# A graph layer on one core: batches of picks over three groups each, in place of three and two in turn

## The chip, the core and the metric

The kernel runs on one core of a Trainium2 chip. A core has five engines with a queue of instructions each: TensorE (PE in the profile, with its weight loads as PEld), VectorE (DVE), ScalarE (ACT), GpSimd (POOL) and SyncE (SP). Here SP only issues DMAs, and GpSimd issues nearly nothing but indirect DMAs, which gather rows of a table by a list of indices. The metric is the time of one execution on the device in microseconds (us), the median of several runs.

## What is computed

One layer of attention over a graph of 6250 nodes with 64 features and 206250 edges, sorted by destination, then a residual sum and a layer norm:

```python
Qh = (x @ Wq.T + bq).reshape(n, H, D)
Kh = (x @ Wk.T + bk).reshape(n, H, D)
Vh = (x @ Wv.T + bv).reshape(n, H, D)
Ee = (edge_attr @ We.T + be).reshape(-1, H, D)
score = (Kh[src] * Qh[dst] * (1.0 / np.sqrt(D)) * Ee).sum(-1)
score = jnp.exp(jnp.clip(score, -5.0, 5.0))
msg = Vh[src] * score[..., None]
wV = jax.ops.segment_sum(msg, dst, num_segments=n)
...
x = _layernorm(x + wV.reshape(n, H * D), axis=-1)
```

with 4 heads of 16 features. For each edge the keys and values of its source node are needed, `Kh[src]` and `Vh[src]`; the sources are random, and this lookup is what the change is about.

## The kernel before

The edges lie in 1612 tiles of 128 (an edge to a partition), 8 tiles to a group: 202 groups, numbered from 0. The main loop runs over the groups. Two groups make a step (the last 8 groups are steps of their own). A preamble makes a table of keys and values in DRAM, `kv_tab`, with a row for each node.

**A group's work.** TensorE transforms the edges' features (`edges`, tile `ee`), fetches the destinations' queries by a product with one-hot rows (`queries`, `qq`), and turns the product of the two (`turn`, `qe`). VectorE multiplies with the keys and sums over a head (`products`: `prod` L811, `score` L813), ScalarE takes the exponential (`weigh`), VectorE weights the values (`message`, L835). TensorE sums a step's messages by destination (`sums`, tile `room`), and VectorE adds the sum into a ring of blocks (`add`, `still` L905). The code of a group mixes the work of several groups: `edges` runs three groups ahead, one-hot rows four.

**Keys and values come in two ways.** Most tiles are gathered: GpSimd issues an indirect DMA for each tile (L295, tile `kv`), four steps ahead of its use, in lots; the first gather of a lot waits for a mark, a place that TensorE must have reached. The other way are the *picks*. For some groups the last two tiles are not gathered. A batch of picks serves four tiles, the last two of each of two adjoining groups. TensorE selects the rows of `x` for the batch's 512 edges by products with one-hot matrices, from a copy of `x` in the on-chip memory (`parts`), and transforms them. A batch goes so:

- `sources` and `second`: ScalarE and VectorE make the row and the remainder of each index (L257 to L259, L678);
- `hots` (L702): VectorE makes the one-hot matrices in seven pieces; pieces 1, 3 and 5 (tile `thin`) are made narrow and widened by ScalarE (L713). Pieces 0 to 5 cover two units of `x` each, piece 6 one unit (the row `hot<-over`);
- `picks`: 50 products of 128x512 on TensorE (tile `pick`), summed in two banks of the accumulator memory;
- `picked`: VectorE merges the two banks into the tile `x` (L728, L729). The next batch's first pick must wait for this, since it overwrites the banks;
- `picked_kv` and `place_kv`: four products with the weights (rows `ee<-w,x`), and two copies by ScalarE into the tiles `kv` (L744).

**What sets the order.** All is emitted by hand in the loop's order, and each engine runs its queue in that order. A list gives the lengths of batches in groups:

```python
LENGTHS = [3, 2]
...
BEGIN = [begin(m) for m in range(LAST)]
READY = [begin(m + 1) - 1 for m in range(LAST)]
```

Batch m runs over groups BEGIN[m] to READY[m]: before, groups 1 to 3, 4 to 5, 6 to 8, 9 to 10 and so on, to group 195. `pieces_of(g)` spreads the seven pieces over the batch's groups: 2, 2 and 3 in a batch of three, 3 and 4 in a batch of two. The picks of a piece are emitted in its group, and its one-hot matrix a group ahead. `picked` stands at the end of group READY[m], and the tiles that the batch serves are those of the groups READY[m] + 4 and READY[m] + 5.

Of the kernel before, what the change touches and what calls it, by code (L numbers as in the profile page):

```python
# [81 lines left out]
PIECES = [(k, min(k + 2, UNITS)) for k in range(0, UNITS, 2)]  # L82
assert PIECES[-1] == (UNITS - 1, UNITS)
WIDE = (1, 3, 5)
LENGTHS = [3, 2]
LEAD = 1
XG = 5

# [1 line left out]
def begin(m):  # L90

    return LEAD + m // len(LENGTHS) * sum(LENGTHS) + sum(LENGTHS[:m % len(LENGTHS)])

# [1233 lines left out]
```

## Time and profile before

| | |
|---|---|
| median of 3 runs | 2004.55 us (1999.72 to 2005.15) |
| the profiled execution | 1987.82 us |
| its span, first to last instruction | 1986.0 us |
| mean granted clock of TensorE | 0.93 |
| rate of the DMAs over the span | 103 GB/s |

The profile is of one execution. It lists each engine's busy time, groups of equal instructions with their busy time, the mean of one, and the engine's idle time ahead of them with what ended it (`<-`). A row of the timeline gives the start and duration in us, the engine, the line, the operation, what it writes and reads, and in brackets how long the engine had idled and what released it. "remote" there is a release that the profile cannot put to an instruction. Windows cut the span at given times and add up each engine's busy time inside.

### The profile page before, as it was taken

How to read it: one execution, taken by the hardware profiler on the slowest of the kernel's cores; microseconds unless marked ns; L12 is line 12 of the kernel's file. 1: busy time of each engine (PE TensorE's matmuls, PEld its weight loads, DVE VectorE, ACT ScalarE, POOL GpSimd, SP SyncE). 2: the span in 40 equal slices, each digit the busy share in tenths (PEclk: the TensorE clock that was granted, in tenths of full speed). 3: DMA queues.
4: the chain of work that ended last, by engine and by line, in shares of the span. 5: the costliest groups of instructions: out<-in, count | busy, mean ns of one | idle time of the engine just before them, and what ended most of it. 6: DMA issues, size and time to landing. Idle time of an engine off the chain costs nothing.

```text
span 1986.0 us, 24370 instructions
## 1 busy us (share of the span) xinstructions
PE 1665.1 (84%) x7369; PEld 1180.0 (59%) x7369; DVE 1515.3 (76%) x2728; ACT 1321.2 (67%) x2047; POOL 1258.1 (63%) x1310
## 2 busy tenths in 40 slices
PE   6467888988888897988788888888888888978995
PEld 5345666666566665666566666666556665656663
DVE  4366878777877786878778787878787877778886
ACT  3356767676666676767666676766766766677774
POOL 6666666666666666666666666666666666666441
PEclk9779999999999899999989999999999999999996
DMA  5543333333333333333333333333333333333320
GB/s 169 166 122 108 105 101 94 111 106 91 105 102 92 108 104 96 102 102 105 102 92 106 99 96 99 101 106 107 92 104 113 101 103 104 92 105 90 111 72 20
DMA packets 116109, 203.60 MB, mean 103 GB/s; under 512 B 54784, under 2 KB 56425, under 8 KB 115855
## 3 DMA queue, kind: packets, MB, share of 16 engines
q1 hardware_dynamic: 73932, 116.94, 20.0%
q0 software_dynamic: 41600, 83.97, 15.5%
q10 hardware_dynamic: 436, 1.04, 0.2%
q8 instruction: 60, 0.98, 0.2%
q14 instruction: 81, 0.66, 0.1%
HBM read 194.25 MB, written 7.59 MB: 102 GB/s over the span
## 4 chain that ended last, share of the span: by engine, by line
PE 52%; DVE 24%; issue 9%; ACT 7%; another core or an unknown queue 5%; DMA 1%; POOL 1%; DVEq 0%; SPq 0%; ACTq 0%; POOLq 0%
PE pick L749 32%; PE ee L749 8%; DVE hot L702 5%; PE room L749 4%; PE qe L780 3%; PE qq L749 3%; DVE x L728 2%; DVE prod L811 2%; DVE qe L835 2%; DVE score L813 2%; DVE msg L855 2%; DVE thin L702 2%; DVE still L905 1%; DMA kv<-kv_tab,src_i 1%
## 5 line engine op out<-in xcount | busy, mean ns | idle before, releaser
L295 POOL DMA_INDIRECT kv<-kv_tab,src_i x1260 | 1218.0, 967 | 671.9 <-issue 289.9
L749 PE MATMUL pick<-hot,parts 128*128 128x512 f32 x3900 | 1140.9, 436 | 123.0 <-DVE x L728 107.6
L749 PEld LDWEIGHTS pick<-hot,parts 128*128 128x128 f32 x3900 | 743.5, 199 | 427.4 <-DVE x L728 140.6
L702 DVE TENSOR_TENSOR hot<-from,still 128x1024 fp32r<-128x1024 bf16 x231 | 280.4, 1214 | 8.2 <-ACT from L257 5.5
L818 ACT ACTIVATE score<-score,five_p 128x32 f32<-128x32 f32 x203 | 64.3, 317 | 310.6 <-DVE score L813 236.7
L749 PE MATMUL ee<-et,we_sb 128*128 128x512 f32 x404 | 218.6, 623 | 46.4 <-ACT kv L744 39.3
L713 ACT ACTIVATE hot<-thin 128x1024 fp32r<-128x1024 bf16 x234 | 245.3, 1048 | 0.1
L849 ACT ACTIVATE msg<-qe 128x512 fp32r<-128x512 f32 (+1 forms) x206 | 122.8, 596 | 166.0 <-DVE qe L835 96.0
L278 ACT ACTIVATE to<-to,one_p 126x1024 bf16<-126x1024 bf16 x198 | 225.8, 1140 | 0.1
L272 ACT ACTIVATE to<-kb,minus_row 126x1024 bf16<-126x1024 uint8 x198 | 225.2, 1137 | 0.0
L728 DVE SCALAR_TENSOR_TENSOR x<-odd,upper,pick 128x512 f32<-128x512 int32 x77 | 57.4, 745 | 199.9 <-PE pick L749 85.4
L780 PE MATMUL qe<-ident,term 128*128 128x128 f32 x806 | 135.4, 294 | 72.0 <-issue 30.0
L760 ACT ACTIVATE eb<-ee,be_col 128x512 f32<-128x512 f32 x202 | 135.8, 672 | 88.7 <-PE pick L749 33.8
L780 PEld LDWEIGHTS qe<-ident,term 128*128 128x128 f32 x806 | 105.4, 152 | 123.9 <-DVE term L774 42.0
L835 DVE SCALAR_TENSOR_TENSOR qe<-weight,kv 128x512 f32<-128x512 f32 x200 | 139.9, 699 | 35.2 <-ACT weight L820 19.4
L702 DVE TENSOR_TENSOR thin<-from,still 128x1024 bf16<-128x1024 bf16 x231 | 157.1, 680 | 0.0
L811 DVE TENSOR_TENSOR prod<-kv,qe 128x512 f32<-128x512 f32 x203 | 136.5, 672 | 19.9 <-remote 10.6
L813 DVE TENSOR_REDUCE score<-prod 128x32 f32<-128x512 f32 x203 | 138.5, 682 | 7.0
L774 DVE TENSOR_TENSOR term<-eb,qq 128x512 f32<-128x512 f32 x202 | 136.6, 676 | 6.5 <-DMA qw<-q_tab 3.3
L855 DVE TENSOR_TENSOR msg<-qe,msg 128x512 fp32r<-128x512 f32 x194 | 132.2, 681 | 3.8 <-ACT eb L760 2.3
L905 DVE TENSOR_REDUCE still<-room 64x64 f32<-64x128 f32 x194 | 57.9, 298 | 95.4 <-PE pick L749 40.0
L749 PEld LDWEIGHTS room<-msg,wide 128*128 128x128 f32 x776 | 114.3, 191 | 25.0 <-issue 11.3
(167 smaller groups left out, 1525.4 us busy)
## 6 DMA issues: line engine op xcount, KB each, us to landing
et<-in_eT SPq DMA_DIRECT2D x100, 512.0 KB
kb<-key_tab SPq DMA_DIRECT2D x101, 252.0 KB
kv<-kv_tab,src_i POOLq DMA_INDIRECT x1260
srcs<-in_src_rows SPq DMA_DIRECT2D x78, 256.0 KB
qw<-q_tab SPq DMA_DIRECT2D x202, 15.8 KB
kv_tab<-kv_sb SPq DMA_DIRECT2D x4, 640.0 KB
q_tab<-q SPq DMA_DIRECT2D x5, 480.0 KB
out<-y SPq DMA_DIRECT2D x2, 512.0 KB
```

The lines of the kernel that those rows point to most:

```text
L272: nc.scalar.activation(TO[g][:, :n, :], KB.pop(g)[:, :n * P].rearrange("p (j e) -> p j e", j=n), AF.Square, bias=minus_row3[:3 * W])
L278: nc.scalar.activation(TO[g][:, :n, :], TO[g][:, :n, :], AF.Relu, bias=one_p[:3 * W], scale=-1.0)
L295: return nc.gpsimd.indirect_dma_start(out=kv_of(g)[:, j, :], out_offset=None, in_=kv_tab[:, :], in_offset=bass.IndirectOffsetOnAxis(ap=src ...
L702: nc.vector.tensor_tensor(to.rearrange("p b (a c) -> p b a c", c=2), pairs((FROM if hi < UNITS else OVER)[m])[:, None].to_broadcast(shape) ...
L713: nc.scalar.activation(*THIN.pop(0), AF.Copy)
L749: mark.append(nc.tensor.matmul(*aps, **kw))
L774: nc.vector.tensor_mul(TERM[g][:, :n], EB.pop(g)[:, :n], qq[:, :n])
L780: nc.tensor.transpose(qe[g % 2][:, 2 * k:2 * k + 2, :], TERM[g][:, k, :], ident)
L811: nc.vector.tensor_mul(prod, kv_of(g)[:, lo:hi, :C], qe[g % 2][:, lo:hi, :])
L813: nc.vector.tensor_reduce(SCORE[g], prod.rearrange("p g (h d) -> p g h d", h=H), axis=AX.X, op=OP.add)
L835: nc.vector.scalar_tensor_tensor(to.rearrange("p g (h d) -> p g h d", h=H), WEIGHT.pop(g)[:, :, :, None].to_broadcast([P, n, H, D]), LEAST ...
L855: nc.vector.tensor_sub(part_of(g, 1)[1], left, part)
```

## The change

One entry of the list of lengths goes:

```diff
 WIDE = (1, 3, 5)
-LENGTHS = [3, 2]
+LENGTHS = [3]
 LEAD = 1
 XG = 5
```

Batches now run over groups 1 to 3, 4 to 6, 7 to 9 and so on, again to group 195. By the count of instructions in the program there are 65 batches in place of 78: 3250 picks on TensorE in place of 3900, and 13 fewer of each instruction that a batch has once. Four tiles for each batch that is gone are gathered instead: 1312 gathers in the main loop in place of 1260, and with the 40 of the preamble 1352 in place of 1300.

**TensorE, second group of the second batch** (group 5), from the queries' product to the next group's first picks. The tiles `pick_758` and `pick_759` are the two banks of the picks; `ee<-et` closes a group. Before:

```order
L749 MATMUL pick_758<-hot,parts 128x512 x2
L749 MATMUL pick_759<-hot,parts 128x512 x2
L749 MATMUL pick_758<-hot,parts 128x512 x2
L749 MATMUL pick_759<-hot,parts 128x512 x2
L749 MATMUL pick_758<-hot,parts 128x512 x2
L749 MATMUL pick_759<-hot,parts 128x512 x2
L749 MATMUL pick_758<-hot,parts 128x512 x2
L749 MATMUL pick_759<-hot,parts 128x512 x2
L749 MATMUL pick_758<-hot,parts 128x512
L749 MATMUL pick_759<-hot,parts 128x512
L749 MATMUL ee<-et,we_sb 128x512
```

The same place after:

```order
L749 MATMUL pick_758<-hot,parts 128x512 x2
L749 MATMUL pick_759<-hot,parts 128x512 x2
L749 MATMUL pick_758<-hot,parts 128x512 x2
L749 MATMUL pick_759<-hot,parts 128x512 x2
L749 MATMUL ee<-et,we_sb 128x512
```

Of the 18 picks that stood here 8 are left; the rest of the batch has moved to group 6.

**VectorE, last group of a batch of three**: before, that of groups 11 to 13, from the add of an earlier step's sum to `x`.

```order
L905 TENSOR_REDUCE still<-room 64x64 x2
L911 SCALAR_TENSOR_TENSOR ring<-still,above,ring 128x64
L914 TENSOR_SCALAR ring<-still,below 128x64
L962 TENSOR_TENSOR y<-y,room 128x128
L702 TENSOR_TENSOR hot<-from,still 128x1024
L835 SCALAR_TENSOR_TENSOR qe_763<-weight,kv_67 128x512
L702 TENSOR_TENSOR thin<-from,still 128x1024
L702 TENSOR_TENSOR hot<-from,still 128x1024
L797 TENSOR_TENSOR of<-still,key 128x1024
L855 TENSOR_TENSOR msg<-qe_763,msg 128x8x64
L728 SCALAR_TENSOR_TENSOR x_760<-odd,upper,pick_758 128x512
```

After, the same stretch in a batch of three that ends in a group of the same kind, groups 7 to 9:

```order
L905 TENSOR_REDUCE still<-room 64x64 x2
L911 SCALAR_TENSOR_TENSOR ring<-still,above,ring 128x64
L914 TENSOR_SCALAR ring<-still,below 128x64
L702 TENSOR_TENSOR hot<-from,still 128x1024
L835 SCALAR_TENSOR_TENSOR qe_763<-weight,kv_70 128x512
L702 TENSOR_TENSOR thin<-from,still 128x1024
L797 TENSOR_TENSOR of<-still,key 128x1024
L855 TENSOR_TENSOR msg<-qe_763,msg 128x8x64
L728 SCALAR_TENSOR_TENSOR x_760<-odd,upper,pick_758 128x512
```

One of the pieces for the next batch (`hot` behind `thin`) no longer stands ahead of `x`: the next batch needs two pieces for its first group, not three.

**GpSimd, the gathers of five steps in a row** (the tiles `kv_66` to `kv_70` are the five buffers of a step). Before:

```order
L295 DMA kv_66<-kv_tab,src_i 128x128 x14
L295 DMA kv_67<-kv_tab,src_i 128x128 x12
L295 DMA kv_68<-kv_tab,src_i 128x128 x12
L295 DMA kv_69<-kv_tab,src_i 128x128 x14
L295 DMA kv_70<-kv_tab,src_i 128x128 x12
```

After:

```order
L295 DMA kv_66<-kv_tab,src_i 128x128 x14
L295 DMA kv_67<-kv_tab,src_i 128x128 x12
L295 DMA kv_68<-kv_tab,src_i 128x128 x14
L295 DMA kv_69<-kv_tab,src_i 128x128 x14
L295 DMA kv_70<-kv_tab,src_i 128x128 x12
```

Of five steps two were gathered with 14 tiles and three with 12; now two of every three have 14. The order of steps, the marks and the lead of four steps are as before.

## The prediction

> **What bounds the kernel now.** I read the engines' totals first, then cut the loop at its own joints. Each batch of picks ends in one VectorE instruction, `x` at L728, in the program's order a fixed place of the batch's last group; its 78 starts are the edges of the windows below.
>
> ```profile
> PE 1665.1 (84%) x7369; PEld 1180.0 (59%) x7369; DVE 1515.3 (76%) x2728; ACT 1321.2 (67%) x2047; POOL 1258.1 (63%) x1310
> PE 52%; DVE 24%; issue 9%; ACT 7%; another core or an unknown queue 5%; DMA 1%; POOL 1%; DVEq 0%; SPq 0%; ACTq 0%; POOLq 0%
> ```
>
> No engine is full, and the chain of work that ended last hops between TensorE and VectorE. The kernel before holds both kinds of batch, so it times the new one itself. First the 37 batches of three groups (first row, the last two, the sum), then the 37 of two (first, last, sum); the columns are the window, its length, and each engine's busy time with its instructions.
>
> ```profile
> core 0: us, PE busy (x) PEld busy (x) DVE busy (x) ACT busy (x) POOL busy (x), PEclk, DMA share, GB/s
> 213.13:239.91 26.78, 23.81 (x111) 16.48 (x109) 21.96 (x38) 17.01 (x27) 17.91 (x19) 0.94 0.36 106
> ...
> 1857.09:1878.28 21.19, 19.59 (x92) 13.74 (x91) 20.62 (x36) 16.33 (x27) 6.95 (x8) 1.00 0.26 78
> 1896.26:1919.82 23.56, 21.34 (x101) 15.05 (x99) 21.87 (x37) 16.92 (x28) 10.06 (x11) 1.00 0.26 79
> sum 1007.88, PE 827.49 PEld 567.51 DVE 800.37 ACT 655.88 POOL 663.66; mean PE 22.36 PEld 15.34 DVE 21.63 ACT 17.73 POOL 17.94
> ```
>
> ```profile
> 194.88:213.13 18.25, 17.44 (x72) 13.15 (x73) 14.84 (x25) 13.82 (x21) 10.51 (x11) 0.86 0.36 99
> ...
> 1878.28:1896.26 17.98, 17.51 (x83) 13.01 (x82) 14.84 (x26) 15.12 (x23) 7.55 (x8) 1.00 0.32 90
> sum 717.06, PE 667.89 PEld 491.43 DVE 563.59 ACT 538.66 POOL 455.09; mean PE 18.05 PEld 13.28 DVE 15.23 ACT 14.56 POOL 12.30
> ```
>
> A batch of three takes 1007.88/37 = 27.24 us, 9.08 a group; one of two takes 717.06/37 = 19.38 us, 9.69 a group. In the short ones TensorE is busy 18.05 of 19.38 us (93%): they are TensorE's. In the long ones it is busy 22.36 of 27.24 (82%) and VectorE 21.63 (79%): something else paces them. Who waits at the joint says what:
>
> ```profile
> 615.97 0.74 DVE L728 SCALAR_TENSOR_TENSOR x<-odd,upper,pick 128x512 f32<-128x512 int32 x1
> 616.76 3.54 PE L749 MATMUL pick<-hot,parts 128*128 128x512 f32 x8 [4.28 <-DVE x L728]
> ...
> 627.80 2.44 PE L749 MATMUL pick<-hot,parts 128*128 128x512 f32 x8
> ...
> 635.23 0.75 DVE L728 SCALAR_TENSOR_TENSOR x<-odd,upper,pick 128x512 f32<-128x512 int32 x1 [3.32 <-PE pick L749]
> ```
>
> ```profile
> 662.67 0.75 DVE L728 SCALAR_TENSOR_TENSOR x<-odd,upper,pick 128x512 f32<-128x512 int32 x1 [5.33 <-remote]
> 663.47 3.78 PE L749 MATMUL pick<-hot,parts 128*128 128x512 f32 x8 [5.20 <-DVE x L728]
> ```
>
> At 615.97 a long batch ends in an odd group: VectorE reaches `x` without idling, late, and TensorE has stood 4.28 us. At 635.23 a short batch ends: VectorE waits 3.32 us for the last pick. At 662.67 a long batch ends in an even group (8, 18, 28 and so on): both stand, VectorE 5.33 us, for a release the profile cannot name. So a long batch wastes TensorE time at its end, for one of two reasons.
>
> **What the change removes and adds.** Batches go from 78 to 65, over the same groups 1 to 195.
>
> ```profile
> L749 PE MATMUL pick<-hot,parts 128*128 128x512 f32 x3900 | 1140.9, 436 | 123.0 <-DVE x L728 107.6 <-issue 9.4 <-DVE x L729 2.6
> L749 PE MATMUL ee<-w,x 128*128 128x128 f32 x624 | 92.8, 293 | 19.8 <-ACT ee L738 11.4 <-issue 6.7 <-ACT eb L760 1.7
> L702 DVE TENSOR_TENSOR hot<-from,still 128x1024 fp32r<-128x1024 bf16 x231 | 280.4, 1214 | 8.2 <-ACT from L257 5.5 <-PE pick L749 2.6
> L702 DVE TENSOR_TENSOR thin<-from,still 128x1024 bf16<-128x1024 bf16 x231 | 157.1, 680 | 0.0
> L702 DVE TENSOR_TENSOR hot<-over,still 128x512 fp32r<-128x512 bf16 x77 | 52.4, 680 | 0.0
> L728 DVE SCALAR_TENSOR_TENSOR x<-odd,upper,pick 128x512 f32<-128x512 int32 x77 | 57.4, 745 | 199.9 <-PE pick L749 85.4 <-remote 61.4 <-issue 18.4
> L729 DVE COPY_PREDICATED x<-second,pick 128x512 f32<-128x512 uint8 x78 | 57.1, 733 | 11.6 <-DVE x L728 1.6 <-issue 1.4 <-remote 1.3
> L678 DVE TENSOR_SCALAR second<-odd,upper 128x512 uint8<-128x512 int32 x77 | 38.0, 494 | 0.0
> L259 DVE TENSOR_SCALAR odd<-srcs 128x512 int32<-128x512 int32 x77 | 36.6, 475 | 0.0
> ```
>
> TensorE: (1140.9 + 92.8)/78 = 15.8 us a batch, times 13 is 206 us gone. VectorE: 3 x 1.214 + 4 x 0.680 + 0.745 + 0.733 + 0.494 + 0.475 = 8.81 us a batch, 115 us gone. ScalarE loses its part of each batch too, and SP 13 loads of index rows; ScalarE is the emptiest of the three and no wait is added anywhere, so I give these nothing. GpSimd gains 52 gathers:
>
> ```profile
> L295 POOL DMA_INDIRECT kv<-kv_tab,src_i x1260 | 1218.0, 967 | 671.9 <-issue 289.9 <-PE pick L749 185.3 <-remote 56.5
> POOL kv L295 <- issue: 289.9, 929, 1.3
> L811 DVE TENSOR_TENSOR prod<-kv,qe 128x512 f32<-128x512 f32 x203 | 136.5, 672 | 19.9 <-remote 10.6
> ```
>
> Each takes 0.967 us and 289.9/929 = 0.312 us of issue, 1.28 us, so 52 add 66 us to GpSimd. What hides them: GpSimd idles 672 us now, of which 290 are issue and the largest other part, 185, are waits at TensorE's picks, the marks that hold it back; and the reader of the gathered rows, `prod`, idles 19.9 us in all its 203 runs, gathers being made four steps ahead. A batch will need 20 gathers, 25.6 us; while batches are longer than that, GpSimd keeps up. Without that cover a batch costs 25.6 us at least.
>
> The totals are only ends (206 us off if TensorE ruled alone, 66 us on if GpSimd did). The sum goes by batches.
>
> (1) Groups 1 to 195 take 39 x (27.24 + 19.38) = 1818 us now; 65 batches of 27.24 us are 1771. **Minus 48 us.** This holds if a long batch after a long one is like a long one after a short one. At L728 it should: in both cases TensorE's next pick waits for `x`, and VectorE stands at the same place of its program.
>
> (2) In the last group of a long batch VectorE now makes the first three pieces for the short batch behind it; after the change it makes two, since the next batch spreads its seven over three groups. One instruction of 1.21 us goes from just ahead of `x`. Where VectorE comes late, as at 615.97, that is time; where it waits anyway, as at 662.67, it is nothing. Of the 65 batches 33 end in odd groups. Bounds 0 and 65 x 1.21 = 79; I take 33 x 1.21. **Minus 40 us.**
>
> (3) New is that each long batch starts where TensorE has stood. The eight first picks took 3.54 us at 616.76 against 2.44 at 627.80: 1.10 us. Bounds 0 and 65 x 1.10 = 72. TensorE has 27.24 - 22.36 = 4.9 us of room in a long batch, so most is absorbed; I take a little over a quarter. **Plus 20 us.**
>
> [...]
>
> Sum: 48 + 40 - 20 = 68 us off a span of 1986.0, that is 1918 of span. The profiled execution took 1987.82, so 1920; against the median of the three runs shown, 2004.55, it is **1937 us**. A batch should then measure 27.24 - 0.61 + 0.31 = 26.9 us.
>
> **Rivals.**
>
> *Long batches get much shorter.* The rows at 1857.09 and 1896.26 are long batches over ordinary groups, but with 8 and 11 gathers: 21.19 and 23.56 us. So the arithmetic alone needs some 22.4 us, and the stand as at 662.67 is not part of it. If that stand comes from the dense short batches ahead, it goes with them, and a batch falls to GpSimd's 25.6: 1818 - 65 x 25.6 = 154 off, 1850 us. Against: it comes in long batches only, while the short ones' waits at `x` have a named release.
>
> *The gathers themselves press, and nothing is gained.* The same two rows read the other way: from 8.8 gathers (mean 8.5 us of GpSimd over 0.967) to 18.55 (17.94 over 0.967), a long batch grew from 22.4 to 27.24, 0.50 us for each. At 20 it would take 27.24 + 0.72 = 27.96 us, and 65 of these are 1817: 2004 us. Against: `prod` hardly waits, and two rows near the program's end are few.
>
> *Slower: every batch starts cold.* If the stand ahead of `x` stays above 4 us at each end and all 1.10 us of term (3) reaches the end, with (2) lost in the same stand, a batch takes 28.34 us: 65 x 28.34 = 1842, 24 on, 2028 us. It decides from 1818/65 = 27.97 us, 0.73 us a batch. For it: the stand at 663.47 (5.20 us, then 3.78 us for eight picks). Against: the 4.9 us of room, and the short batches, which now start behind such stands, keep 93% busy all the same.
>
> That the change does not do what it says is excluded by the program's order, shown above: 13 batches fewer and 52 gathers more.
>
> **How the numbers follow.** Forecast 0.57; its own range, from terms (2) and (3) at their ends taken in part, 1905 to 1975. Much shorter 0.16 (1850 to 1905). Nothing gained 0.13 (1975 to 2015). Cold starts 0.09. Other losses, such as gathers that eat up their lead, 0.05. A measurement here can tell some 0.3% (6 us) from no change. Faster: 0.57 + 0.16 + 0.02 of the third case = 0.75; within 0.3%: 0.10; slower: 0.01 + 0.09 + 0.05 = 0.15. The range leaves out cold starts, the other losses and the far end of the short batches (0.05): 1865 to 2005.
>
> **What would show it.** Step (1): the windows between starts of L728 average near 26.9 us, 65 of them; TensorE's total is down by some 200 us, VectorE's by 115, GpSimd's up by 50. (2): at odd ends `x` still starts without idle, closer behind the last pick. (3): the first eight picks of batches take 3.5 us where TensorE stood over 4 us. Gathers still hidden: `prod` idles no more than some 20 us in all. The forecast is wrong if windows average 28 or more, or if they fall to 25.6 with GpSimd standing at no marks.

## The result, and the profile after

The changed kernel took **2053.85 us** (median of 4 runs, 2051.14 to 2057.35) beside 2004.54 for the kernel before: a ratio of 1.026 (95% interval 1.0242 to 1.0276). It is slower by 49 us, where 68 us of gain were forecast, and it lies above the range. One thing has to be said ahead of the experiments: in three of the six sets of runs on the chip (three of the five in the section below) the kernel before itself took 1742 to 1745 us in place of 2004 to 2007. The two are called the level of 2004 and the level of 1744. A time is compared within its set, or between sets of one level; in the three sets at the level of 2004 the kernel before took 2004.54, 2006.74 and 2004.76 us.

First the engines' totals and the chain of work that ended last, from the changed kernel's page (at the level of 2004, like the profile before):

```profile
PE 1578.9 (77%) x6615; PEld 1095.7 (53%) x6615; DVE 1418.8 (69%) x2585; ACT 1257.5 (61%) x1943; POOL 1299.6 (63%) x1362
PE 42%; DVE 21%; issue 15%; another core or an unknown queue 10%; ACT 10%; DMA 1%; POOL 1%; DVEq 0%; SPq 0%; ACTq 0%; POOLq 0%
```

TensorE lost 754 of its instructions but only 86 us of busy time; its granted clock, the mean share of its full speed, fell from 0.930 to 0.881. The chain has less TensorE (42% for 52%) and more of what the profile cannot name: 25% under "issue" and "unknown queue", where it was 14%. Then the windows from one start of `x` (L728) to the next, cut as for the prediction (the first two of 61 and their sum; window, length, busy time of each engine with its instructions):

```profile
core 0: us, PE busy (x) PEld busy (x) DVE busy (x) ACT busy (x) POOL busy (x), PEclk, DMA share, GB/s
206.16:237.46 31.30, 26.03 (x108) 17.93 (x108) 19.03 (x31) 17.71 (x27) 20.56 (x22) 0.83 0.27 81
237.46:264.34 26.88, 21.80 (x90) 14.88 (x90) 21.75 (x42) 15.88 (x26) 17.98 (x19) 0.90 0.36 105
...
sum 1775.01, PE 1400.99 PEld 969.20 DVE 1257.65 ACT 1121.61 POOL 1149.80; mean PE 22.97 PEld 15.89 DVE 20.62 ACT 18.39 POOL 18.85
```

A batch takes 1775.01/61 = **29.10 us**, 9.70 a group; forecast were 26.9, and before it was 46.62 for five groups, 9.32 a group. The groups of instructions whose waits moved (busy time, mean ns of one | idle time just before them and what ended it):

```profile
L295 POOL DMA_INDIRECT kv<-kv_tab,src_i x1312 | 1260.3, 961 | 699.7 <-issue 303.3 <-PE pick L749 127.7 <-remote 119.8
L749 PE MATMUL ee<-et,we_sb 128*128 128x512 f32 x404 | 241.8, 682 | 154.3 <-ACT kv L744 140.8 <-issue 13.2 <-ACT eb L760 0.2
L811 DVE TENSOR_TENSOR prod<-kv,qe 128x512 f32<-128x512 f32 x203 | 136.9, 674 | 134.4 <-remote 49.4 <-PE pick L749 33.6 <-PE room L749 21.2
L728 DVE SCALAR_TENSOR_TENSOR x<-odd,upper,pick 128x512 f32<-128x512 int32 x64 | 47.7, 746 | 188.3 <-remote 117.4 <-PE pick L749 24.4 <-PE room L749 23.0
L744 ACT ACTIVATE kv<-ee 128x256 f32<-128x256 f32 x130 | 42.6, 380 | 164.2 <-issue 152.5 <-remote 10.8 <-PE ee L749 0.8
```

The rows of `ee<-et` and of the placing in the kernel before:

```profile
L749 PE MATMUL ee<-et,we_sb 128*128 128x512 f32 x404 | 218.6, 623 | 46.4 <-ACT kv L744 39.3
L744 ACT ACTIVATE kv<-ee 128x256 f32<-128x256 f32 x156 | 50.7, 378 | 33.0 <-PE pick L749 20.2 <-remote 7.8 <-PE room L749 4.0
```

`prod` (L811) idled 19.9 us before and 134.4 now. ScalarE idles 164.2 us ahead of the rows' placing (`kv<-ee`, L744), where it was 33.0. Most of it stands under "issue". TensorE idles 154.3 us ahead of `ee<-et`, where it was 46.4, mostly for that placing. One such stand, in order of time (start, length, engine and what it does, idle time ahead of it):

```profile
706.70 0.60 PE L780 MATMUL qe<-ident,term 128*128 128x128 f32 x4
...
707.25 0.94 POOL L295 DMA_INDIRECT kv<-kv_tab,src_i  x1 [0.30 <-issue]
...
707.83 1.16 PE L749 MATMUL ee<-w,x 128*128 128x128 f32 x8 [0.19 <-ACT ee L738]
708.50 0.94 POOL L295 DMA_INDIRECT kv<-kv_tab,src_i  x1 [0.31 <-issue]
...
708.74 2.11 PE L749 MATMUL pick<-hot,parts 128*128 128x512 f32 x8
...
709.75 0.94 POOL L295 DMA_INDIRECT kv<-kv_tab,src_i  x1 [0.30 <-issue]
...
711.00 1.00 POOL L295 DMA_INDIRECT kv<-kv_tab,src_i  x1 [0.30 <-issue]
...
712.30 0.95 POOL L295 DMA_INDIRECT kv<-kv_tab,src_i  x1 [0.30 <-issue]
714.42 0.94 POOL L295 DMA_INDIRECT kv<-kv_tab,src_i  x1 [1.17 <-remote]
717.11 0.69 DVE L811 TENSOR_TENSOR prod<-kv,qe 128x512 f32<-128x512 f32 x1 [5.23 <-remote]
717.26 0.94 POOL L295 DMA_INDIRECT kv<-kv_tab,src_i  x1 [1.90 <-remote]
717.29 0.66 ACT L744 ACTIVATE kv<-ee 128x256 f32<-128x256 f32 x2 [5.32 <-issue]
...
718.00 1.22 PE L749 MATMUL ee<-et,we_sb 128*128 128x512 f32 x1 [7.15 <-ACT kv L744]
```

By the records TensorE has turned `qe` at 707.30 and made `ee<-w,x` at 708.99. Yet `prod`, which needs that `qe`, starts at 717.11, and the placing, which needs that `ee`, at 717.29, ten and eight microseconds later; both wait for TensorE's semaphore, a counter that instructions on TensorE raise. The trace records five increments of it between 717.00 and 717.22, though TensorE had ended its last work at 710.85; the gather ahead of them had ended at 715.36. So TensorE stands from 710.85 to 718.00 for its own late signal. Meanwhile GpSimd issues gathers, one every 1.25 us, until it needs a signal of TensorE too. It isn't waiting for rows: those that this `prod` reads were gathered 76 us earlier, and VectorE's sequencer, which waits at the gathers' semaphores ahead of `prod`, never stood there longer than 50 ns, by the view of that line (count: least, median and longest ns):

```profile
L811 DVEq EVENT_SEMAPHORE  x656: 21/50/50, 153.1 to 2044.5; - x164
```

One thing about the waits is new. The placing's sequencer now waits at gathers' semaphores 121 times; in the kernel before it was twice. The likely reason is that the picked tiles no longer keep fixed places in the buffers, so that a placing overwrites a place that was gathered before. The placing does not stand for these gathers. Where it waits for a gather alone, it waits 17 ns at the most. Of its 50 waits of over 0.3 us, each at a gather's semaphore and TensorE's together, 44 end within 0.1 us behind a recorded increment of TensorE's and only 2 behind one of the gather's.

### The profile page after: what moved, and what is told of

Read it like the earlier page. It is cut to its first block, busy times and chain, and to the rows that moved or that the text cites. A ratio compares the mean times of both kernels' runs of the same rounds, so it can differ in the third digit from the quotient of the medians.

```text
span 2055.6 us, 22732 instructions
## 1 busy us (share of the span) xinstructions
PE 1578.9 (77%) x6615; PEld 1095.7 (53%) x6615; DVE 1418.8 (69%) x2585; ACT 1257.5 (61%) x1943; POOL 1299.6 (63%) x1362
## 4 chain that ended last, share of the span: by engine, by line
PE 42%; DVE 21%; issue 15%; another core or an unknown queue 10%; ACT 10%; DMA 1%; POOL 1%; DVEq 0%; SPq 0%; ACTq 0%; POOLq 0%
PE pick L749 24%; PE ee L749 9%; DVE hot L702 3%; PE room L749 3%; PE qe L780 3%; DVE prod L811 2%; DVE qe L835 2%; DVE score L813 2%; PE qq L749 2%; DVE x L728 2%; DVE term L774 1%; ACT kv L744 1%; DVE msg L855 1%; DVE still L905 1%
## 5 line engine op out<-in xcount | busy, mean ns | idle before, releaser
L295 POOL DMA_INDIRECT kv<-kv_tab,src_i x1312 | 1260.3, 961 | 699.7 <-issue 303.3
L749 PE MATMUL pick<-hot,parts 128*128 128x512 f32 x3250 | 1034.2, 461 | 130.0 <-DVE x L728 107.8
L749 PEld LDWEIGHTS pick<-hot,parts 128*128 128x128 f32 x3250 | 652.9, 210 | 428.4 <-DVE x L728 138.5
L749 PE MATMUL ee<-et,we_sb 128*128 128x512 f32 x404 | 241.8, 682 | 154.3 <-ACT kv L744 140.8
L702 DVE TENSOR_TENSOR hot<-from,still 128x1024 fp32r<-128x1024 bf16 x192 | 232.7, 1212 | 0.0
L811 DVE TENSOR_TENSOR prod<-kv,qe 128x512 f32<-128x512 f32 x203 | 136.9, 674 | 134.4 <-remote 49.4
L713 ACT ACTIVATE hot<-thin 128x1024 fp32r<-128x1024 bf16 x195 | 204.3, 1048 | 0.0
L780 PE MATMUL qe<-ident,term 128*128 128x128 f32 x806 | 139.9, 301 | 82.7 <-DVE term L774 46.3
L728 DVE SCALAR_TENSOR_TENSOR x<-odd,upper,pick 128x512 f32<-128x512 int32 x64 | 47.7, 746 | 188.3 <-remote 117.4
L749 PEld LDWEIGHTS ee<-et,we_sb 128*128 128x128 f32 x404 | 73.0, 208 | 180.3 <-ACT kv L744 156.0
L744 ACT ACTIVATE kv<-ee 128x256 f32<-128x256 f32 x130 | 42.6, 380 | 164.2 <-issue 152.5
```

Of the source, the lines that this page charges most:

```text
L295: return nc.gpsimd.indirect_dma_start(out=kv_of(g)[:, j, :], out_offset=None, in_=kv_tab[:, :], in_offset=bass.IndirectOffsetOnAxis(ap=src ...
L702: nc.vector.tensor_tensor(to.rearrange("p b (a c) -> p b a c", c=2), pairs((FROM if hi < UNITS else OVER)[m])[:, None].to_broadcast(shape) ...
L713: nc.scalar.activation(*THIN.pop(0), AF.Copy)
L749: mark.append(nc.tensor.matmul(*aps, **kw))
L780: nc.tensor.transpose(qe[g % 2][:, 2 * k:2 * k + 2, :], TERM[g][:, k, :], ident)
L811: nc.vector.tensor_mul(prod, kv_of(g)[:, lo:hi, :C], qe[g % 2][:, lo:hi, :])
```

## The experiments

Three theories were set against each other. **A**: a long batch behind a long one is dear in itself. **B**: the gathers set the pace (46.62 us for 32 gathers are 1.457 us each, 29.10 for 20 are 1.455). **C**: with a period of three groups the picked tiles lose their fixed places in the ten groups of `kv` buffers, and new waits follow.

### Other lengths, fewer gathers (level of 2004; the kernel before 2006.74 us)

```diff
-LENGTHS = [3]
+LENGTHS = [3, 3, 2, 2]
```

> Batches of 3, 3, 2 and 2 groups in turn: as many batches (78) and gathers (1300) as in the kernel before, in another order. The changed kernel's windows average 29.10 us, where a batch of three had 27.24 and one of two 19.38 in the kernel before, 46.62 for five groups. Theory A (a batch costs more behind a long batch): half of the batches of three now stand behind one of three, so 19 or 20 of them cost 29.10 in place of 27.24; if a batch of two behind one of two costs 19.38 as ever, the time is 2004 + 19.5 x 1.86 = 2040 us. Theory B (the gathers set the pace: 46.62 us for 32 gathers is 1.457 us each, 29.10 for 20 is 1.455): as many gathers, 2004 us. Theory C (with a period of three groups the picked tiles no longer fall on fixed places of the ten groups that the kv buffers hold, and other waits follow from it): the period is ten groups here, places are fixed, 2004 us.

Measured: 2011.74 us, 1.003 (1.0009 to 1.005). Theory A asked for 2040 and falls; the order of lengths hardly matters.

```diff
-LENGTHS = [3]
+LENGTHS = [2]
-LAST = max(m for m in range(1, NG) if begin(m) - 1 + 5 < NG)
+LAST = max(m for m in range(1, NG) if begin(m) - 1 + 6 < NG)
```

> 97 batches of two groups each, 4850 picks and 1224 gathers. Theory A (a batch costs by its length and what stands before it, and short ones leave no stand): 97 x 19.38 = 1880 us against 38.8 x 46.62 = 1809 for the same 194 groups in the kernel before, so some 71 us above it: 2075 us. Theory B (the gathers pace the loop): 12 gathers a batch x 1.456 = 17.5 us, below TensorE's busy 18.05 of a short batch, so TensorE paces: 97 x 18.05 = 1751, some 58 us below the kernel before at the best: 1946 to 2075 us. Theory C (places in the kv buffers): fixed places, so as theory A, 2075 us.

Measured: 1955.82 us, **0.976** (0.9731 to 0.9797): faster than both kernels, with 950 picks more than before and 76 gathers less. That is in theory B's range (1946 to 2075) and below the 2075 of A and C.

```diff
-LENGTHS = [3]
+LENGTHS = [3, 3, 4]
```

> Batches of 3, 3 and 4 groups in turn: 59 batches and 1376 gathers, 68 to ten groups, and a period of ten groups, so that the picked tiles have fixed places in the kv buffers, unlike in the changed kernel. Theory B (gathers at 1.456 us each): 68 x 1.456 = 99.0 us for ten groups against 93.24 in the kernel before, 19.5 times: 112 us above it, 2117 us. Theory C (only the places matter): batches of three back at 27.24, one of four some 35.1 (27.24 + 7.86, the step from two to three): 89.6 us, 71 us below the kernel before, 1933 us. Theory A (a batch is dear behind a long one): 2 x 29.10 + 37 = 95.2 us, 38 us above, 2042 us.

Measured: 2107.61 us, 1.050 (1.0474 to 1.0526). Theory B had 2117, C 1933 and A 2042: the fixed places don't help, and C falls.

```diff
         for j in js:
+            if j == 0 and g >= 2 * KVB:
+                continue
             ins = gather_kv(g, j)
```

> The changed kernel without the gather of the first tile of each group from group 10 on: 192 gathers of 1312 left out (those tiles keep old rows), every other instruction as it was, 17 gathers a batch in place of 20. Theory B at full price (1.455 us a gather): 2054 - 279 = 1775 us, if nothing else ends a batch first; at the price that the tail's batches gave (0.50 us each): 1958 us. Theories A and C: gathers are off the path (the awaited ones are 70 us old), 2054 us less nothing, at most some 10 us.

Measured: 1808.29 us. The 192 gathers were worth 2053.85 - 1808.29 = 246 us (the changed kernel is of the set before), **1.28 us each**, just about GpSimd's whole time for one (0.961 us and some 0.30 ahead of it). So B holds at nearly its full price (it had 1775 us), for rows that are read 70 us later.

### One half of the change at a time (at the level of 1744; the kernel before 1744.66 us)

The added half alone, a gather into an unread tile behind one of the kernel before, and the removed half alone, the changed kernel without 52 gathers:

```diff
             ins = gather_kv(g, j)
...
+            if j == 0 and g >= 10 and (g - 10) * 52 // 192 < (g - 9) * 52 // 192:
+                nc.gpsimd.indirect_dma_start(
+                    out=junk, out_offset=None, in_=kv_tab[:, :],
+                    in_offset=bass.IndirectOffsetOnAxis(ap=src_i[:, g * G:g * G + 1], axis=0))
```

> The kernel before, with 52 gathers more (spread over the groups from 10 on, into a tile that nobody reads); batches and picks as they were. It is the added half of the change alone. Theory B (each gather costs the loop its 1.30 us, as the 192 left out gave: 2054 to 1805): 2004 + 52 x 1.30 = 2072 us. Theory A (a row of long batches is dear in itself, gathers are hidden as I predicted): 2004 us. Half a price, 0.50 us, would give 2030.

```diff
+            if j == 0 and g >= 10 and (g - 10) * 52 // 192 < (g - 9) * 52 // 192:
+                continue
             ins = gather_kv(g, j)
```

> The changed kernel without 52 of its gathers (those tiles keep old rows; all else as it was): the removed half of the change alone, 13 batches fewer at 1300 gathers. Theory B: 2054 - 52 x 1.30 = 1986 us, so that 13 batches less are worth 18 us and not the 206 us of TensorE in them. Theory A: 2054 us.

GpSimd kept busy with other work (iota, an instruction that writes a row of rising numbers; the run's page has it at 0.33 us each and lists no DMA of it), and gathers that wait for no pick:

```diff
+            if j == 0 and g >= 2 * KVB:
+                for k in range(4):
+                    ins = nc.gpsimd.iota(junk, pattern=[[1, 224]], base=0, channel_multiplier=1)
...
+                continue
             ins = gather_kv(g, j)
```

> The changed kernel with the 192 gathers of the first tiles left out (those tiles keep old rows), and in the place of each, behind the same mark, four small iota of GpSimd into a tile that nobody reads (0.32 us each by the profile, 1.29 together, a gather's time). Theory G (GpSimd's time paces the loop, whatever it does in it): 2054 us, as with the gathers. Theory D (it is what a gather does beyond occupying GpSimd, its descriptors or its transfer, that slows the others): 1805 us, as without them.

```diff
-            ins = gather_kv(g, j)
-            if j == js[0]:
-                behind(ins, after)
+            gather_kv(g, j)
```

> The changed kernel without the marks: no gather waits for a pick any more, only for its buffer and its lane. Theory M (GpSimd and TensorE pace each other through the marks): GpSimd no longer stands at them (some 250 us of its idle time), the loop falls to what TensorE and the waits at the joints need, 1800 to 1900 us. Theory D (a gather costs the loop its 1.30 us wherever it stands): the gathers are the same 1352, 2054 us within some 20, or more where they now come in rows.

Measured beside 1744.66 us: 52 gathers more 1744.04 (ratio 1.0002, 0.9988 to 1.0015); 52 less 1668.73 (0.957); iota 1804.56 (1.034); no marks 1734.35 (0.995). None of the expectations, which were worked out from 2004, can be read here; at this level other things bind. In the last three, all with three groups a batch, GpSimd is busy 1254.4 us (52 less), 1304.2 (no marks) and 1375.0 (iota), and the span less that time is 413, 428 and 429 us. So with such batches **GpSimd's time sets the pace** at this level, whatever GpSimd does in it. With the kernel before's batches 52 gathers more cost nothing.

### The same at the level of 2004 (the kernel before 2004.76 us)

> The changed kernel itself, beside the kernel before. The second set of runs ran at another level than the first (the kernel before 1744.66 us there, 2006.74 in the first), so every expectation from here on has two numbers. Theory S (signals): at the level of 2004 TensorE's semaphore increments reach the others only where GpSimd pauses between gathers, so a batch takes 1.25 us for each of its gathers and some 4 us of pauses; at the level of 1744 they come 0.04 us after TensorE's end, and GpSimd or TensorE binds, whichever is longer. At 2004: 2054 (1.026). At 1744: GpSimd binds with 20 gathers a batch, 1668.7 (52 gathers less) + 52 x 1.25 = 1734 us (0.994). My forecast's theory (TensorE and the joints) has no place for a level.

> Batches of two groups throughout. Theory S at the level of 2004: as before, 0.976. At 1744: TensorE binds (a short batch took 18.56 us there beside long ones, 12 gathers need 15.0): 97 x 18.4 = 1785 against 39 x 41.46 = 1617, so some 165 us above the kernel before, 1910 us (1.09).

> The kernel before with 52 gathers more. Theory S at the level of 2004: each costs its full 1.25 to 1.30 us, 2004 + 66 = 2070 (1.033). Theory A: 2004 (1.000). At 1744: 1744 (1.000), as measured.

> The changed kernel with four iota of GpSimd in place of each of 192 gathers. At the level of 2004: if any work of GpSimd keeps TensorE's signals back, 2054 (1.025); if only gathers do, 1805 (0.90), as without them. At 1744: 1804 (1.034), as measured, GpSimd's time.

Measured: the changed kernel 2055.36 (1.0252, 1.0217 to 1.0288), batches of two 1959.42 (0.977), 52 gathers more **2074.69** (1.033, 1.0292 to 1.0367), iota for gathers **1820.55** (0.908). The two bold ones decide. Gathers that nobody reads cost 70 us, 1.34 each. The 192 times four iota take about as much of GpSimd's time as 192 gathers, yet the run with them is only 12 us longer than the one in which those gathers were left out (1820.55 against 1808.29, in another set; by their ratios, 0.908 and 0.900, it is some 18). So at this level a gather's price is neither its data nor GpSimd's time, but something that a gather does to the others and an iota doesn't. And the change is taken apart: 70 us for 52 gathers, and 2055.36 - 2074.69 = -19 us for its 13 batches less. This takes the added gathers first; the other order, the changed kernel without 52 gathers, ran at the level of 1744 alone.

The windows of the kernel before with 52 gathers more (the start of `x` is at L733 there), the sums of 37 batches of three and of 37 of two:

```profile
sum 1047.67, PE 832.55 PEld 567.33 DVE 801.30 ACT 648.50 POOL 680.69; mean PE 22.50 PEld 15.33 DVE 21.66 ACT 17.53 POOL 18.40
sum 764.93, PE 692.17 PEld 504.50 DVE 566.07 ACT 547.20 POOL 479.96; mean PE 18.71 PEld 13.64 DVE 15.30 ACT 14.79 POOL 12.97
```

28.32 + 20.67 = 48.99 us for five groups in place of 46.62, with the same instructions on TensorE. No placing waits for a gather in this run, and it lost 70 us all the same. GpSimd's groups in the run with iota, and in the one that left the gathers out and put nothing there:

```profile
L296 POOL DMA_INDIRECT kv<-kv_tab,src_i x1120 | 1072.8, 958 | 374.4 <-issue 263.7 <-PE pick L756 33.7 <-PE ee L756 12.4
L322 POOL IOTA junk<- 128x224 int32 x768 | 253.1, 330 | 40.8
```

```profile
L295 POOL DMA_INDIRECT kv<-kv_tab,src_i x1120 | 1082.1, 966 | 632.3 <-issue 231.0 <-PE pick L751 134.9 <-PE ee L751 74.6
```

GpSimd idled 632.3 us without the iota and 374.4 ahead of its gathers with them (and 40.8 ahead of the iota): 217 of the 253.1 us of iota went into time in which it had stood. So most of this work, which is no gather, found room in GpSimd's pauses.

### What a gather holds up, and the changed kernel at the level of 1744

```diff
+        if g >= 2 * KVB:
+            return nc.gpsimd.indirect_dma_start(
+                out=kv_of(g)[:, j, :C], out_offset=None, in_=kv_tab.rearrange("n (u c) -> (n u) c", u=2),
+                in_offset=bass.IndirectOffsetOnAxis(ap=src_i[:, t:t + 1], axis=0))
         return nc.gpsimd.indirect_dma_start(
```

> The changed kernel with gathers of half rows (256 bytes in place of 512, into the k half of each tile; from group 10 on the v half stays old and the rows are others), as many and as often. If a gather's price is its issue: 2055 us at the level of 2004 (1.025). If it is the bytes moved, half the price of 1160 gathers goes, some 0.65 us each: below 1800 (0.85 to 0.90). At the level of 1744: 1734 (0.994) by GpSimd's time, either way.

> The changed kernel without marks: gathers wait for their buffers alone. Theory S in its strict form (TensorE's increments get through only where GpSimd pauses) at the level of 2004: GpSimd now runs a step's 13 gathers, 17 us, without a pause, and everybody stands in that time; the two groups' work behind it needs 15 us more, so 32 us a step in place of 19.4, a time of 2700 us or more. Theory M (the marks themselves tie GpSimd to TensorE): GpSimd's pauses at the marks, some 4 us a batch, go: 2055 - 65 x 4 = 1795 us. At the level of 1744: 1734 (0.994), as measured.

```diff
                 for i, lot in enumerate(going):
                     gather((lot, where[i * len(where) // len(going)]))
+                    if g - 1 in READY and i == 3:
+                        for k in range(6):
+                            nc.gpsimd.iota(junk, pattern=[[1, 224]], base=0, channel_multiplier=1)
```

> The changed kernel with a pause of GpSimd in the first group of each batch behind its fourth gather: six iota in a row, 2 us, in which no gather is issued; nothing is left out. Theory S at the level of 2004: TensorE's increments get through there, so the stand at the rows' placing (164 us of ScalarE's idle time in all) shrinks, and GpSimd stands less later: 2055 or below, down to some 1960. If GpSimd's time paces as such: 2055 + 65 x 2.0 = 2185. At the level of 1744: GpSimd's time, 1734 + 130 = 1864 (1.07).

> The changed kernel. At the level of 2004: 2055 (1.025), as measured twice. At the level of 1744: GpSimd binds, 20 gathers of 1.25 us a batch: 1734 us (0.994), as with half rows (1732) and without marks (1734), which both leave GpSimd its 1312 gathers.

> Batches of two groups throughout. At the level of 2004: 0.977, as measured twice. At the level of 1744: TensorE binds, 97 x 18.4 = 1785 against 39 x 41.46 = 1617 for as many groups in the kernel before: 1910 us (1.09).

> The changed kernel without marks. At the level of 2004: 2700 us or more if TensorE's increments got through only in GpSimd's pauses; 1795 if the marks alone tied the two together; 2055 if the marks do not matter. At the level of 1744: 1734 (0.994), as measured twice.

Both sets ran at the level of 1744 (the kernel before 1742.11 and 1742.72). Half rows 1732.35 (0.993), no marks 1734.2 and 1733.17 (0.995 both times), pause 1873.82 (1.075), the changed kernel 1733.43 (**0.994**, 0.9926 to 0.9959), batches of two 1914.97 (**1.099**, 1.097 to 1.1006). Each is within 10 us of what was expected for this level. What they were to tell at the level of 2004 stays open: a gather of half the bytes, gathers without marks, and a pause of GpSimd at a chosen place never ran there.

The changed kernel at this level, its page's totals, then the sum of its 61 windows:

```profile
PE 1470.6 (85%) x6615; PEld 1032.3 (60%) x6615; DVE 1411.9 (81%) x2585; ACT 1250.2 (72%) x1943; POOL 1306.0 (75%) x1362
PE 33%; DVE 23%; DMA 19%; ACT 11%; issue 9%; POOL 5%; DVEq 0%; POOLq 0%; SPq 0%; ACTq 0%
```

```profile
sum 1515.38, PE 1303.07 PEld 910.18 DVE 1250.81 ACT 1119.04 POOL 1151.46; mean PE 21.36 PEld 14.92 DVE 20.51 ACT 18.34 POOL 18.88
```

and the groups that stood above, from the same run:

```profile
L295 POOL DMA_INDIRECT kv<-kv_tab,src_i x1312 | 1266.4, 965 | 399.9 <-issue 183.5 <-DMA kv<-kv_tab,src_i 107.3 <-PE pick L749 51.5
L811 DVE TENSOR_TENSOR prod<-kv,qe 128x512 f32<-128x512 f32 x203 | 137.2, 676 | 149.1 <-DMA kv<-kv_tab,src_i 92.3 <-PE pick L749 28.8 <-PE room L749 13.5
L728 DVE SCALAR_TENSOR_TENSOR x<-odd,upper,pick 128x512 f32<-128x512 int32 x64 | 47.5, 742 | 55.4 <-PE pick L749 55.3
L744 ACT ACTIVATE kv<-ee 128x256 f32<-128x256 f32 x130 | 41.9, 377 | 0.8 <-PE ee L749 0.8
```

A batch takes 1515.38/61 = 24.84 us, 20 gathers at 1.24. ScalarE idles 0.8 us in all ahead of the placing, where it was 164.2. The unknown queue is gone from the chain, "issue" is 9% for 15%, and `prod` now waits for a releaser with a name, the gathers, whose lead is used up. Batches of two, the windows' sums at the levels of 2004 and of 1744 (93 each):

```profile
sum 1711.54, PE 1660.03 PEld 1216.04 DVE 1518.78 ACT 1294.65 POOL 1057.37; mean PE 17.85 PEld 13.08 DVE 16.33 ACT 13.92 POOL 11.37
```

```profile
sum 1707.65, PE 1658.77 PEld 1217.16 DVE 1520.59 ACT 1294.91 POOL 1063.84; mean PE 17.84 PEld 13.09 DVE 16.35 ACT 13.92 POOL 11.44
```

18.40 and 18.36 us, TensorE busy 17.85 and 17.84: TensorE binds, and the loop takes the same time at both levels. The ratio differs because the kernel before takes 2004.76 us at one and 1742.72 at the other.

Last, TensorE's semaphore increments, counted from the traces: how many of the program's increments the trace records, then, between 200 and 1650 us, the bursts, how long after the last gather's end they came, and the pauses. A burst is four or more increments within 0.45 us behind a silence of over 1 us; a pause is a gap of over 0.85 us between two gathers:

```
                      level  recorded      bursts  since the last gather's end   pauses
before                2004   1704 of 2219    74    0.94 to 2.65 us               131
changed               2004   1752 of 2235    70    0.89 to 2.48                  129
before, 52 more       2004   1786 of 2219    81    0.91 to 2.72                  126
batches of two        2004   1862 of 2297    45    0.95 to 1.47                  192
iota for gathers      2004   1669 of 2233    44    0.98 to 1.65                  165
changed               1744   2231 of 2235     0    -                               0
before, 52 more       1744   2213 of 2219     0    -                               0
batches of two        1744   2296 of 2297     0    -                             196
```

At the level of 2004 the bursts all lie between gathers, 0.89 us or more behind a gather's end, though in the first four runs only 8 to 9% of the time lies more than 0.85 us behind one. Single increments come during gathers too, but fewer: in the changed kernel's trace 43% of the recorded ones fall in those 8% of the time. At the level of 1744 there are no bursts, with pauses or without. GpSimd's pause often ends with the burst it waits for, so the first four rows alone don't say which causes which. The run with iota does: in all of its 44 bursts the last instruction that GpSimd had begun is an iota, and 21 of them begin while an iota runs. In 43 of them GpSimd goes on to its next instruction within 0.4 us, so it waits for nobody, and the signals get through.

## Why the prediction was wrong

**The step that failed is the cover of the gathers.** "GpSimd idles 672 us now", "`prod` idles 19.9 us", so 52 gathers are hidden "while batches are longer than" 25.6 us. Off the data path they were, but not free: at the level of 2004 52 gathers cost 70 us, 1.34 each. GpSimd's idle time was room for iota but not for gathers, because there TensorE's signals come late while GpSimd gathers (their bursts lie 0.89 us or more behind a gather's end), and the others stand for them. The windows of that level can be written as 1.25 us for each gather and a rest: 40.0 + 6.6 us for five groups before, 25.0 + 4.1 for a changed batch, 21.25 + 4.0 with three gathers less (1542.08/61 = 25.28). The bursts of TensorE's signals lie in that rest. What in a gather holds the signals up, no run shows.

**Step (1), minus 48 us, failed with it.** "A long batch after a long one is like a long one after a short one": it took 29.10 us and not 27.24. The long batch before was not a thing of its own. The same batches in another order changed the time by 0.3%, and 46.62 us for 32 gathers are the same price of a gather as 29.10 for 20 (1.457 and 1.455 us). This fits one budget of waits that both kinds of batch share; the two equal prices alone don't prove it.

**Step (2), minus 40 us, did not come.** At odd ends `x` was to start without idling. Counted from its rows, VectorE idles 2.36 us on average ahead of `x` at the 31 odd ends of those windows, where at the 19 odd ends of long batches it had idled 0.44 us. The instruction ahead of it did go; the signal it waits for comes later by more.

**Step (3), plus 20 us, had the right sign.** TensorE's busy time a batch rose from 22.36 to 22.97 us with about the same work, 0.6 us where 0.31 were taken, and 65 times 0.6 is 40 us of the batches' length at the most. The granted clock goes with the stands at `ee<-et`: 0.930 with 46.4 us of them in the kernel before, 0.881 with 154.3 here, and 0.948 with 52.4 for this same program at the level of 1744. So the lower clock is taken as a consequence of the stands; no run changed it alone. In the trace of the kernel before, the eight picks behind a stand of 2.18 us or more took 0.55 to 0.65 us each on average in all 23 cases, and 0.42 behind four of the stands that were shorter (1.23 to 1.74 us). By these cases a stand of 4.28 us that the 1.21 us of step (2) shorten, to 3.07 us, would still be followed by slow picks.

**What was taken at nothing.** "No wait is added anywhere" is not so: the placing's 121 waits at gathers' semaphores are new. They cost next to nothing by themselves, as shown above.

**The rivals.** "The gathers themselves press" was the mechanism, with too small a price: 0.50 us for each, read from two windows near the end, against 1.28 to 1.34 measured. With 1.3 us the same working, 27.24 + 1.45 x 1.3 = 29.1 us, gives the measured batch; the 1.3 us is known only from the runs after it. It had a chance of 0.13, argued down because "`prod` hardly waits": `prod` shows only whether rows come late, not what issuing them does to others. "Every batch starts cold" gave 2028, slower too, but by another mechanism: the slow picks behind stands, measured at 0.6 us a batch at the most, and not late signals. "Much shorter" named GpSimd's 25.6 us as the floor, and at the level of 1744 a batch does lie near it (24.84 us), with a ratio of 0.994.

**What was right:** 13 batches less are a gain, though of 19 us where the two steps had 88. VectorE's total fell by 97 us and GpSimd's rose by 42 (115 and 50 were given); TensorE's fell by 86 and not by 200: a pick took 461 ns on average, where it had been 436, at a granted clock of 0.881 for 0.930.

No version that ran at both levels and computes the whole result beat both kernels at both: batches of two take 0.976 at one and 1.099 at the other.

## What to carry to other kernels

Work that nobody waits for by data can still be dear: price it once by leaving some of it out, and once by adding some that nobody reads (here 1.28 and 1.34 us a gather), before calling it hidden by its engine's idle time. Two kinds of batch that alternate can share their waits, so the mean of one kind is no safe price for a loop made of it alone (27.24 us in turn with short ones, 29.10 alone). The sum over the period, divided by each thing that is counted in it, gives a rival price for each (here 1.457 us a gather, which the windows of the kernel before already held). And measure the kernel before in every set: a change that trades one engine for another can have either sign where the level differs (batches of two: 0.976 and 1.099).

## What the runs showed that I had not expected

The same program has two levels, 2004 and 1744 us, that go with the set of runs and not with the kernel. At the upper one TensorE's signals come late: a consumer that waits starts 0.04 us behind TensorE's recorded end at its best, and often 3 to 10 us; at the lower one, in the kernel before with 52 gathers more, VectorE and ScalarE start 0.04 to 0.09 us behind it at the picks, the sums and the edges, and its page puts all 107.4 us of VectorE's idle time ahead of `x` down to the last pick. So the recorded end is not the signal: at the stand shown above TensorE's last work ends at 710.85, and five increments are recorded 6.15 us and more behind it. Which part of the way is late, no run here shows.

What sets the level is open: the chip, its condition, or the recording. The chip's number alone doesn't: of the sets above, the one of other lengths ran at the level of 2004 and the next at 1744, both on the chip of number 8. One sign of the level is that 19 to 25% of TensorE's semaphore increments are missing from the record at 2004 and 0.3% or less at the other. Whether the recording holds TensorE back at the upper level, no run shows.

At the level of 2004 GpSimd's gathers go with late signals of TensorE and its iota do not, while a gather's pitch is 1.25 us at both levels (0.94 and 0.30). Whether half the bytes would hold them half as long was not settled.
